# A two-layer graph network with masked attention: one cyclic order by hand for all engines, norms on ScalarE, adj turned straight from DRAM

## The chip, the cores and the metric

The kernel runs on one core of a Trainium2 chip. A core has TensorE (PE in the profile; PEld are its weight loads), VectorE (DVE), ScalarE (ACT), GpSimd (POOL) and SyncE (SP), which here only issues DMAs. Each engine executes its own instructions in the order in which they were put into its stream, and waits on semaphores for what other engines or DMAs have to deliver. The metric is the time of one launch on the device in microseconds, the median of several runs.

## The reference

There are B = 64 independent elements. Each has a matrix x of N = 256 tokens by F = 512 features, and adj, 256 by 256, non-negative and mostly zero. All is float32. Two layers are applied, each followed by a residual sum and a layer norm without learned factors:

```python
# layer 0
deg = sum(adj, axis=-1)
agg = einsum('bij,bjf->bif', adj, x) / maximum(deg, 1e-6)
x   = layernorm(x + relu(concatenate([x, agg]) @ W0.T))
# layer 1: 8 heads of 64
q, k, v = x @ Wq.T + bq, x @ Wk.T + bk, x @ Wv.T + bv
scores  = einsum('bhqd,bhkd->bhqk', q, k) * 64 ** -0.5
attn    = softmax(scores * (adj + adj))
x       = layernorm(x + (attn @ v) @ Wo.T + bo)
```

The kernel computes adj·(x·W) instead of (adj·x)·W in layer 0. The division by the degree belongs to a row of the sum, so it can be applied to the rows of adj beforehand or to the rows of the product afterwards.

## The kernel before

**Tiling.** A tile has 128 partitions (P). The 256 tokens of an element are NT = 2 groups of 128, the 512 features FC = 4 groups of 128. Tokens are put on the partitions in an order of blocks of L = 32[...]: a full transpose is made of a DMA that moves the blocks to their places and a VectorE transpose inside them.

**Products.** The four big projections (L for layer 0, Q for queries and keys, V for values, O for the output) are each done by a seven-product scheme of Winograd's kind (`winograd`): two blocks of tokens by two blocks of features, seven block products, numbered 1 to 7, instead of eight. The sums of weight blocks are made once (`sum_blocks`, L125). The sums of token blocks are made per element by GpSimd (`token_sums`, L214): s1 to s4, in tiles named sums. The products run in the order 5, 1, 3, 6, 2, 7, 4 into three PSUM accumulators, called c, a and b (p0c, p0a, p0b for L; pq, pv, po for Q, V, O). An accumulator goes on being added to after a part has been copied out: product 3 adds onto c after product 5 was copied out of it, 6 onto a after 1, 7 after 6, and 4 after the result of 7 was joined. So TensorE has to wait for each of these copies (`keep`: ScalarE for L, Q, V; VectorE for O, L489) and of the joins (`join`, VectorE, L236).

In the profile, one product of 128 by 512 in float32 is two MATMUL rows; one of the seven steps of L has 4 rows, of Q 16, of V and O 4 of half the width.

**Stages of an element b.**

- `prepare`: turn x (z_x to xT, L274), its token sums, degree and 1/degree (L280 to L283), adj scaled row by row by 1/degree (`an`, L286), written to DRAM (way_a, L185) and fetched back turned by blocks (z_a, L193), then turned by VectorE into aT (L197).
- `project0` and `layer0`: the L products into oy, of which one half is x·W and the other is to be multiplied by adj; two neighbour sums pm (L323) of four wide products together; add (L327), relu and residual (L328), layer norm (`layer_norm`, L171 to L181) into x1; x1 goes to DRAM (way_x) and comes back twice: turned (`turn1`) and plain, as rest (`fetch_x1`), to which GpSimd adds the bias (L342).
- `queries_keys`, `values`: Q and V.
- `attend`: for each of four pairs of heads, scores sc (L416), times adj into s (L428), maximum of each row (L435), four exponentials on ScalarE with a running sum (L438), reciprocal (L446), four scalings by it on VectorE (L448), a transpose of the blocks (L205), out to DRAM (way_s, L207) and back as sT (L209).
- `context`: attention times v (pc, L462), copied to ctxT (L469), token sums of it.
- `project1`, `finish`: O, the second layer norm, output in eight DMAs (L498).

A layer norm takes the statistics on VectorE (L174, L176), adds epsilon and takes the power -1/2 on GpSimd (L178, L180), and applies both on VectorE (L181).

**Order.** `iteration(i)` (L502) works on several elements at once: scores of element i, layer 0 of i + 2, queries, keys and values of i + 1, output of i - 1, preparation of i + 3. Only TensorE's order is written by hand (L541): its instructions run in the order in which the program names them. For VectorE, ScalarE, GpSimd and the DMA queue on SP the framework's scheduler picks the order, by priorities and its own estimates. All DMAs of the loop leave from the one queue on SP. Most tiles have between two and four buffers[...].

Of the kernel before, what the change touches and what calls it, by code (L numbers as in the profile page):

```python
# [7 lines left out]
F32 = mybir.dt.float32  # L8
# [6 lines left out]
DEG_EPS = 1e-6  # L15


@with_exitstack
def kernel(
# [29 lines left out]

    nc = tc.nc  # L50
# [7 lines left out]
    A = P // L  # L58

# [8 lines left out]
    def bank(name):  # L68
        return banks.tile([P, F], F32, tag="ps", name=name)

    def token_rows(tile, dram, a):

        rows = dram.rearrange("(a t l) f -> a l t f", a=A, t=NT)
        return tile[a * L : (a + 1) * L], rows[a]

    xs, adjs, zxs = {}, {}, {}
    loaded = set()

    def load_turned(b):
        if b >= B or b in loaded:  # L80
            return
        loaded.add(b)
        zxs[b] = sb.tile([P, A, NT, F // A], F32, tag="z", name=f"z_x_{b}", bufs=3)
        for a in range(A):
            nc.sync.dma_start(
                out=zxs[b][a * L : (a + 1) * L].rearrange("m b t k -> m (b t) k"),
                in_=x[b, :, a * P : (a + 1) * P].rearrange("(g m) k -> m g k", m=L),
            )

    def load_rows(tiles, dram, b, tag, bufs):  # L90
        if b >= B or (tag, b) in loaded:
            return
        loaded.add((tag, b))
        tiles[b] = sb.tile([P, NT, dram.shape[2]], F32, tag=tag, name=f"{tag}_{b}", bufs=bufs)
        for a in range(A):
            dst, src = token_rows(tiles[b], dram[b], a)
            nc.sync.dma_start(out=dst, in_=src)
# [12 lines left out]
    def load_blocks(queue, dst, dram, swapped=False, natural=False):  # L110

        for blk, kh, nh in ((B11, 0, 0), (T3, 0, 1), (B21, 1, 0), (B22, 1, 1)):
            nh ^= swapped
            cols = dram[:, nh * G : (nh + 1) * G]
            if natural:
                rows = cols.rearrange("(c p) o -> p c o", p=P)
                queue.dma_start(out=dst(slice(None), blk), in_=rows[:, 2 * kh : 2 * kh + 2])
                continue
            rows = cols.rearrange("(a c l) o -> a l c o", a=A, c=FC)
            for a in range(A):  # L120
                queue.dma_start(
                    out=dst(slice(a * L, (a + 1) * L), blk), in_=rows[a, :, 2 * kh : 2 * kh + 2]
                )
# [5 lines left out]
    load_turned(0)  # L129
    load_blocks(nc.scalar, lambda p, k: w0[p, k, :, 1], w0t[F:])  # L130
    load_blocks(nc.sync, lambda p, k: w0[p, k, :, 0], w0t[:F])
    for b in range(2):
        load_turned(b)
        load_rows(adjs, adj, b, "adj", 4)
        load_rows(xs, x, b, "x", 3)
    bqk = const.tile([P, 2, FC], F32, name="bqk")
    nc.scalar.dma_start(out=bqk[:, 0], in_=bq)
    nc.scalar.dma_start(out=bqk[:, 1], in_=bk)
    bvT = const.tile([P, FC], F32, name="bvT")
    nc.scalar.dma_start(out=bvT, in_=bv.rearrange("o (c p) -> p (o c)", p=P))  # L140
    bo_sb = const.tile([P, F], F32, name="bo_sb")
    nc.scalar.dma_start(out=bo_sb, in_=bo.to_broadcast([P, F]))
    load_blocks(nc.sync, lambda p, k: wo[p, k], wot, natural=True)
    load_blocks(nc.sync, lambda p, k: wqk[p, k, :, 0], wqt, swapped=True)
    load_blocks(nc.sync, lambda p, k: wqk[p, k, :, 1], wkt, swapped=True)
    load_blocks(nc.sync, lambda p, k: wv[p, k], wvt)
    sum_blocks(nc.vector, w0.rearrange("p k c m o -> p k (c m o)"))

    def later_weights():
# [3 lines left out]
        sum_blocks(nc.vector, wqk.rearrange("p k c m o -> p k (c m o)"))  # L153

        bv_all = sb.tile([P, FC, P], F32, tag="h", name="bv_all", bufs=3)
        nc.vector.tensor_copy(bv_all, bvT.unsqueeze(2).to_broadcast([P, FC, P]))
        ps = bank("p_bv")
# [11 lines left out]
        sum_blocks(nc.gpsimd, wv.rearrange("p k c o -> p k (c o)"))  # L169

    def layer_norm(dst, src, tag):  # L171

        stats = small.tile([P, 6], F32, tag="stats", name=f"stats_{tag}")
        nc.vector.bn_stats(stats, src)  # L174
        mv = small.tile([P, 2], F32, tag="mv", name=f"mv_{tag}")
        nc.vector.bn_aggr(mv, stats)  # L176
        ve = small.tile([P, 1], F32, tag="ve", name=f"ve_{tag}")
        nc.gpsimd.tensor_scalar(ve, mv[:, 1:2], LN_EPS, None, ALU.add)  # L178
        rstd = small.tile([P, 1], F32, tag="rstd", name=f"rstd_{tag}")
        nc.gpsimd.tensor_tensor(rstd, ve, neg_half, ALU.pow)  # L180
        nc.vector.tensor_scalar(dst, src, mv[:, 0:1], rstd, ALU.subtract, ALU.mult)  # L181

    def outward(src, C, tag):
        way = bounce.tile([NT * A, L, A * C * L], F32, tag=f"way{C}", name=f"way_{tag}", bufs=5)
        nc.sync.dma_start(out=way.rearrange("(t b) m k -> (b m) t k", t=NT), in_=src)  # L185
        return way

    def transposed(dst, way, tag):

        C = dst.shape[1]  # L190
        z = sb.tile([P, NT, A, C * L], F32, tag="z", name=f"z_{tag}", bufs=3)
        for a in range(A):
            nc.sync.dma_start(  # L193
                out=z[a * L : (a + 1) * L].rearrange("m t b k -> m (t b) k"),
                in_=way[:, :, a * C * L : (a + 1) * C * L].rearrange("g m k -> m g k"),
            )
        nc.vector.transpose(  # L197
            dst.rearrange("p c t (b m) -> p (t b) c m", m=L),
            z.rearrange("p t b (c l) -> p (t b) c l", l=L),
        )  # L200

    def transposed_s(dst, s, tag):

        flat = s.rearrange("p a c r l -> p (a c r l)")
        nc.vector.transpose(flat, flat)  # L205
        way = bounce.tile([A, L, A, NT * 2 * NT * L], F32, tag="way_s", name=f"way_{tag}", bufs=4)
        nc.sync.dma_start(out=way.rearrange("b l a k -> (b l) (a k)"), in_=flat)  # L207
        for a in range(A):
            nc.sync.dma_start(  # L209
                out=dst[a * L : (a + 1) * L].rearrange("l b c r m -> l b (c r m)"),  # L210
                in_=way[:, :, a].rearrange("b l k -> l b k"),
            )

    def token_sums(src, tag):  # L214


        def block(t, kh):
            return src[:, 2 * kh : 2 * kh + 2, t]

        sums = sb.tile([P, 4, 2, P], F32, tag="sums", name=f"sums_{tag}", bufs=3)  # L220
        s1, s2, s3, s4 = (sums[:, k] for k in range(4))
        nc.gpsimd.tensor_tensor(s1, block(1, 0), block(1, 1), ALU.add)  # L222
        nc.gpsimd.tensor_tensor(s2, s1, block(0, 0), ALU.subtract)
        nc.gpsimd.tensor_tensor(s3, block(0, 0), block(1, 0), ALU.subtract)
        nc.gpsimd.tensor_tensor(s4, block(0, 1), s2, ALU.subtract)
        return {1: block(0, 0), 2: block(0, 1), 3: s4, 4: block(1, 1), 5: s1, 6: s2, 7: s3}
# [3 lines left out]
    def winograd(multiply, keep, part, psums):  # L230


        pa, pb, pc = psums

        def join(ps, t, n):
            nc.vector.tensor_tensor(part(t, n), ps, part(t, n), ALU.add)  # L236

        multiply(5, pc, True)
        keep(pc, 1, 1)
        yield  # L240
        multiply(1, pa, True)
        keep(pa, 0, 0)
        yield
        multiply(3, pc, False)
        yield
        multiply(6, pa, False)
        keep(pa, 0, 1)
        yield
        join(pc, 0, 1)
        multiply(2, pb, True)  # L250
        join(pb, 0, 0)
        yield
        multiply(7, pa, False)
        join(pa, 1, 1)
        yield
        multiply(4, pa, False)
        keep(pa, 1, 0)
        yield

    def by_turns(order, works):  # L260

        for name in order:
            if name in works:
                next(works[name])

    xTs, aTs, x1Ts, qks, vs, sTs, cTs = {}, {}, {}, {}, {}, {}, {}
    xSs, x1Ss, cSs, ways, rests = {}, {}, {}, {}, {}

    def prepare(b):

        xT = sb.tile([P, FC, NT, P], F32, tag="xT", name=f"xT_{b}")
        z = zxs.pop(b)
        for t in range(NT):
            nc.vector.transpose(  # L274
                xT[:, :, t].rearrange("p c (b m) -> p b c m", m=L),
                z[:, :, t].rearrange("p b (c l) -> p b c l", l=L),
            )
        xSs[b] = token_sums(xT, f"x_{b}")
        deg = small.tile([P, NT], F32, tag="deg", name=f"deg_{b}")
        nc.vector.tensor_reduce(deg, adjs[b], AX.X, ALU.add)  # L280
        nc.vector.tensor_scalar(deg, deg, DEG_EPS, None, ALU.max)
# [3 lines left out]
        for t in range(NT):  # L285
            nc.vector.tensor_scalar(an[:, t], adjs[b][:, t], rdeg[:, t : t + 1], None, ALU.mult)  # L286
# [292 lines left out]
```

## Time and profile before

| | before |
|---|---|
| median of 3 runs | 3511.33 us (3509.74 to 3514.02) |
| span of the profiled execution | 3508.7 us |
| instructions | 51138 |
| TensorE's granted clock, mean | 0.989 |
| DMA | 530.14 MB, 58.2% of the 16 engines' span for the queue on SP |

After its start the program runs in equal turns, one for each element. To read it, the turn is the unit: what each engine does in a turn, where TensorE stands still in it, and what ended that. In the rows of groups, the columns are line, engine, operation, output and input, shapes, number of instructions, then busy time and mean duration in ns, then the idle time of the engine ahead of them and what ended it.

### The profile page before, as it was taken

Reading aid. Unit: us, or ns where it says so; the run is one execution under the profiler, and the core shown is the slowest. Engines: PE = TensorE matmul, PEld = TensorE weight load, DVE = VectorE, ACT = ScalarE, POOL = GpSimd, SP = SyncE. Lnnn points to the kernel's source line nnn. Section 1 sums busy time; section 2 is a strip of 40 time slices with the busy share of each in tenths; the row PEclk is TensorE's granted clock in tenths of the full one; section 3 lists DMA queues with packets and bytes.
Section 4 is the critical chain, followed back from the end, with each engine's and each line's share of the span. In section 5 each row is a group of like instructions: output and inputs, shape, how many; then the busy total and the mean of one; then the engine's idle time right before and its main releaser. Section 6 shows DMA issues by size and latency. Waiting matters only on the chain.

```text
span 3508.7 us, 51138 instructions
## 1 busy us (share of the span) xinstructions
PE 3185.1 (91%) x17168; PEld 2216.8 (63%) x17168; DVE 2692.0 (77%) x4943; ACT 1083.1 (31%) x3713; POOL 952.1 (27%) x1421
## 2 busy tenths in 40 slices
PE   4989999999999999999999999999999999999996
PEld 2665665666666666656656656666666666566565
DVE  4668778787787787787787787877877877877875
ACT  0323333233232332332333332332323323333332
POOL 2222231331322322322322313313223223223222
PEclk8999999999999999999999999999999999999998
DMA  5555655655665565556556556656655665565554
GB/s 149 133 135 141 158 157 143 159 155 146 158 158 150 156 157 154 153 148 159 157 143 158 156 143 160 153 149 157 159 150 155 155 157 153 146 158 156 143 136 130
DMA packets 519686, 530.14 MB, mean 151 GB/s; under 512 B 119936, under 2 KB 420992, under 8 KB 519424
## 3 DMA queue, kind: packets, MB, share of 16 engines
q1 hardware_dynamic: 517184, 525.55, 58.2%
q8 instruction: 137, 2.24, 0.3%
q10 hardware_dynamic: 2240, 1.32, 0.2%
q14 instruction: 125, 1.02, 0.1%
HBM read 308.55 MB, written 218.10 MB: 150 GB/s over the span
## 4 chain that ended last, share of the span: by engine, by line
DVE 34%; PE 33%; ACT 8%; POOL 7%; issue 6%; SPq 5%; DMA 5%; DVEq 0%; ACTq 0%; POOLq 0%
PE p0a L301 7%; ACT s L438 7%; DVE s L428 7%; PE pqa L355 7%; DVE nmax L435 6%; DVE s L448 5%; PE pqc L355 4%; PE p0b L301 3%; POOL rstd L180 3%; DMA way_a<-an 2%; DVE stats L174 2%; PE sc L416 2%; DVE x1T L197 2%; SPq L209 2%; PE pva L384 2%
## 5 line engine op out<-in xcount | busy, mean ns | idle before, releaser
L438 ACT ACTIVATE s<-s,nmax 128x256 f32<-128x256 f32 x1024 | 507.6, 497 | 609.1 <-DVE nmax L435 609.1
L371 ACT ACTIVATE qk<-pqa,bqk 128x128 f32<-128x128 f32 x768 | 219.0, 368 | 842.2 <-PE pqa L355 842.2
L222 POOL TENSOR_TENSOR sums_x<-x1T 128x256 f32<-128x256 f32 x64 | 46.7, 729 | 1453.7 <-DVE rtotal L446 1378.1
L448 DVE TENSOR_SCALAR s<-s,rtotal 128x256 f32<-128x256 f32 x1024 | 393.4, 446 | 6.5
L355 PE MATMUL pqc<-sums_x,wqk 128*128 128x128 f32 x2048 | 259.1, 280 | 98.8 <-POOL sums_x L222 98.7
L428 DVE TENSOR_TENSOR s<-sc,adj 128x512 f32<-128x512 f32 x512 | 327.9, 681 | 27.0 <-PE sc L416 26.9
L355 PEld LDWEIGHTS pqc<-sums_x,wqk 128*128 128x128 f32 x2048 | 247.0, 194 | 153.2 <-POOL sums_x L222 148.5
L205 DVE STREAM_TRANSPOSE s<-s 128x1024 f32<-128x1024 f32 x256 | 317.8, 1241 | 6.3
L301 PE MATMUL p0c<-w,sums_x 128*128 128x512 f32 x512 | 253.6, 618 | 73.4 <-ACT oy L314 59.4
L435 DVE TENSOR_REDUCE nmax<-s 128x4 f32<-128x1024 f32 x256 | 312.2, 1219 | 8.5
L178 POOL TENSOR_SCALAR ve<-mv 128x1 f32<-128x1 f32 x256 | 56.9, 222 | 871.9 <-DVE mv L176 871.9
L181 DVE TENSOR_SCALAR x<-oy,mv,rstd 128x512 f32<-128x512 f32 x128 | 124.6, 974 | 217.5 <-POOL rstd L180 217.5
L301 PE MATMUL p0a<-w,sums_x 128*128 128x512 f32 x512 | 246.9, 604 | 24.2 <-ACT oy L314 24.2
L323 PE MATMUL pm<-oy,aT 128*128 128x512 f32 x512 | 238.6, 609 | 31.1 <-DVE aT L197 29.5
L416 PE MATMUL sc<-qk 64*128 64x256 f32 x2048 | 255.2, 389 | 0.0
L355 PEld LDWEIGHTS pqa<-x1T,wqk 128*128 128x128 f32 x2048 | 248.4, 192 | 10.3 <-DVE qk L236 3.9
L462 PE MATMUL pc<-sT,v 128*64 128x256 f32 x2048 | 250.6, 386 | 3.7 <-DMA sT<-way_s 3.7
L355 PEld LDWEIGHTS pqa<-sums_x,wqk 128*128 128x128 f32 x2048 | 248.6, 192 | 6.5
L355 PE MATMUL pqa<-x1T,wqk 128*128 128x128 f32 x2048 | 249.8, 275 | 2.5 <-DVE qk L236 2.5
L355 PE MATMUL pqa<-sums_x,wqk 128*128 128x128 f32 x2048 | 249.3, 275 | 0.0
L301 PE MATMUL p0a<-w,xT 128*128 128x512 f32 x512 | 247.3, 605 | 1.6 <-DVE oy L236 1.6
L416 PEld LDWEIGHTS sc<-qk 64*128 64x128 f32 x2048 | 187.4, 186 | 88.7 <-issue 71.6
(89 smaller groups left out, 5351.2 us busy)
## 6 DMA issues: line engine op xcount, KB each, us to landing
way_s<-s SPq DMA_DIRECT2D x256, 512.0 KB, 3.2
sT<-way_s SPq DMA_DIRECT2D x1024, 128.0 KB, 3.9
z_x<-in_x_dram SPq DMA_DIRECT2D x256, 128.0 KB, 3.9
x<-in_x_dram SPq DMA_DIRECT2D x256, 128.0 KB, 2.7
way_x<-x SPq DMA_DIRECT2D x64, 512.0 KB, 3.1
z_x<-way_x SPq DMA_DIRECT2D x256, 128.0 KB, 3.1
rest<-way_x SPq DMA_DIRECT2D x64, 512.0 KB, 5.8
out_dram<-h SPq DMA_DIRECT2D x512, 64.0 KB, 1.7
```

The source lines that it names most:

```text
L181: nc.vector.tensor_scalar(dst, src, mv[:, 0:1], rstd, ALU.subtract, ALU.mult)
L205: nc.vector.transpose(flat, flat)
L301: nc.tensor.matmul(ps, lhsT=left[k][:, c], rhs=w0[:, WEIGHTS[k], c], start=start and c == 0, stop=True, skip_group_check=True,)
L323: nc.tensor.matmul(ps, lhsT=aT[:, j, t], rhs=oy[:, 1, j], start=(j == 0), stop=(j == NT - 1))
L355: nc.tensor.matmul(ps[:, m, j], lhsT=wqk[:, WEIGHTS[k], c, m, j * P : (j + 1) * P], rhs=left[k][:, c], start=start and m == j == c == 0, s ...
L371: nc.scalar.activation(part(t, n)[:, m, j], ps[:, m, j], AF.Identity, bias=bqk[:, m, c : c + 1])
L416: nc.tensor.matmul(scs[hp, j][:, t], lhsT=qk[d, 0, hp, t * P : (t + 1) * P], rhs=qk[d, 1, hp].rearrange("d (t b m) -> d b t m", t=NT, m=L) ...
L428: nc.vector.tensor_tensor(rows[:, j * NT : (j + 1) * NT], scs[hp, j].rearrange("p t (k l) -> p t k l", l=L), aj.rearrange("p t (k l) -> p ...
L435: nc.vector.tensor_reduce(nmax, rows, AX.XY, ALU.max, negate=True)
L438: nc.scalar.activation(rows[:, r], rows[:, r], AF.Exp, bias=nmax[:, r : r + 1], accum_out=total[:, r : r + 1],)
L448: nc.vector.tensor_scalar(rows[:, r], rows[:, r], rtotal[:, r : r + 1], None, ALU.mult)
L462: nc.tensor.matmul(ps[j * D : (j + 1) * D, n], lhsT=vs[b][:, c, h * D : (h + 1) * D], rhs=sT[:, :, c, j * NT : (j + 1) * NT].rearrange("p ...
```

## The change

Four things change together.

1. **One cyclic order by hand.** The stages become named steps, and a table `PLAN` lists them in the order in which every engine gets them. Each entry is a step and an offset: `L5+2` is product 5 of L for element i + 2. All engines and the DMA queue are now ordered by hand (`tc.manual_schedule()` without a list of engines): an engine's instructions run in the order of the table, whatever is ready earlier. The rows of the table begin with a step of TensorE; the other steps in a row belong to other engines. TensorE's own order changes as well: the scores of the four pairs of heads are spread (Sa, Sb; Sc, Sd), and the neighbour sums AY0, AY1 come ahead of Q.
2. **Norms and softmax scaling move to ScalarE.** The four scalings of each pair of heads (step na to nd) and the four applications of a layer norm (AYn, ln) become ACTIVATEs with a scale, and for the norms a bias, for each partition. GpSimd makes the bias, one more small operation for each norm.
3. **adj is turned straight from DRAM** (step Dza), without `an` and its way through DRAM; 1/degree is applied when the neighbour sum is added (AYa).
4. **Buffers.** x, xT, z, s, sT, sums and h1 get names of their own with one buffer each; adj has four, v two, the DRAM tiles for x1 five. The output leaves in four DMAs. Of the weights, those of the queries load from ScalarE's queue.

The names of the steps: S scores, m times adj, M maximum, e and f exponentials, r reciprocal, n scaling, T transpose, Dw and Ds out to DRAM and back, C context and c its copy; Lk, Qk, Vk, Ok copies and Lj, Qj, Vj, Oj joins of a product; AY neighbour sum, AYa add and relu, AYb statistics, AYp factors, AYn norm; lb, lp, ln the same of the last norm; xS, yS, cS token sums; Dx, Dzx, Dza, Dadj loads; Dway, Dz1, Drest the ways of x1.

The core of the diff:

```diff
+PLAN = """
+    Sa+0 c0-1 lp1-2 Dx+2
+    Sb+0 ma+0 xS2+2
+    L5+2 ln1-2 Dsd-1 Ma+0 xS4+2
+    L1+2 Lk5+2 x1T+1 Dsc-1 ea+0 mb+0
+    L3+2 yS1+1 Dza+3 Lk1+2 yS2+1 fa+0 Mb+0 yS4+1
+    L6+2 lb0-2
+    L2+2 Lk6+2 lp0-2 eb+0 bo-1
+    L7+2 Lj2+2 fb+0 Lj3+2 ra+0
+    Sc+0 Lj7+2 na+0
+    Sd+0 mc+0
+    L4+2 ln0-2 rb+0 md+0 Dout-2
+    C1a-1 Lk4+2 Mc+0 nb+0
+    C1b-1
+    AY0+2 Md+0 ec+0
+    AY1+2 AYa0+2 fc+0 AYb0+2
+    Q5+1 ed+0 rc+0 Ta+0 c1-1
+    V5+1 AYa1+2 cS1-1 Qk5+1
+    Q1+1 cS2-1 AYb1+2 cS4-1 Vk5+1
+    V1+1 Qk1+1 Tb+0 cS3-1
+    Q3+1 yS3+1 Vk1+1 Dwb+0 AYp0+2 Dwa+0 nc+0 Dadj+4
+    O5-1 AYp1+2
+    Q6+1 Tc+0
+    O1-1 Ok5-1 Qk6+1
+    Q2+1 Ok1-1 Dsb+0 fd+0 Qj3+1
+    V3+1 Dsa+0 AYn0+2 rd+0 Qj2+1
+    Q7+1 nd+0
+    O3-1 Qj7+1 AYn1+2
+    V6+1 Td+0 Dway+2
+    Q4+1 Vk6+1 deg+4 xT0+3
+    O6-1 Qk4+1 Vj3+1
+    V2+1 Ok6-1 xT1+3
+    O2-1 Dz1+2 xS3+3
+    V7+1 xS1+3
+    O7-1 Vj7+1 Dwd+0 Dwc+0
+    V4+1 Oj7-1 Oj2-1
+    O4-1 Vk4+1 aT+3
+    C0a+0 Ok4-1 Vj2+1 Drest+0
+    C0b+0 Oj3-1 Dzx+4 lb1-1
+"""
...
-        nc.vector.tensor_scalar(dst, src, mv[:, 0:1], rstd, ALU.subtract, ALU.mult)
+    def norm_factors(name, b):
+        mv = held[f"mv_{name}", b]
+        nc.gpsimd.tensor_scalar(mv[:, 1:2], mv[:, 1:2], LN_EPS, None, ALU.add)
+        nc.gpsimd.tensor_tensor(mv[:, 1:2], mv[:, 1:2], neg_half, ALU.pow)
+        nc.gpsimd.tensor_scalar(mv[:, 0:1], mv[:, 0:1], mv[:, 1:2], -1.0, ALU.mult, ALU.mult)
+    def norm_apply(name, b, dst, src):
+        mv = held[f"mv_{name}", b]
+        nc.scalar.activation(dst, src, AF.Identity, bias=mv[:, 0:1], scale=mv[:, 1:2])
...
-        an = sb.tile([P, NT, N], F32, tag="h", name=f"an_{b}", bufs=3)
-        for t in range(NT):
-            nc.vector.tensor_scalar(an[:, t], adjs[b][:, t], rdeg[:, t : t + 1], None, ALU.mult)
-        transposed(aTs[b], outward(an, NT, f"a_{b}"), f"a_{b}")
+    @step("Dza")
+    def _(b):
+        z = tile_of("za", b, [P, A, NT, N // A])
+        for a, part in groups():
+            nc.sync.dma_start(
+                out=z[part].rearrange("m b t k -> m (b t) k"), in_=turned_rows(adj[b], a, N // A)
+            )
...
-            nc.vector.tensor_tensor(h, ps, h, ALU.add)
+            nc.vector.scalar_tensor_tensor(h, held[f"AY{t}", b], rdeg, h, ALU.mult, ALU.add)
...
-                nc.vector.tensor_scalar(rows[:, r], rows[:, r], rtotal[:, r : r + 1], None, ALU.mult)
+                nc.scalar.activation(
+                    rows(b)[:, r], rows(b)[:, r], AF.Identity, scale=of("total", b)[:, r : r + 1]
+                )
...
-    with tc.manual_schedule(engines={mybir.EngineType.PE}):
-        for i in range(-3, B + 1):
-            iteration(i)
+    with tc.manual_schedule():
+        run("Dzx", 0)
+        first_weights()
+        run("Dza", 0)
+        run("Dadj", 0)
+        run("Dx", 0)
+        run("Dadj", 1)
+        run("Dadj", 2)
+        run("Dzx", 1)
+        more_loads()
+        for i in range(-6, B + 6):
+            for name, ahead in plan:
+                if name == "Q5" and i + ahead == 0:
+                    later_weights()
+                if name == "bo" and i + ahead == 0:
+                    last_weights()
+                run(name, i + ahead)
```

## The prediction

> **What bounds the kernel now.** I read the busy shares first, then TensorE's timeline over one turn of the loop, then the table of waits, then the price rows.
>
> ```profile
> PE 3185.1 (91%) x17168; PEld 2216.8 (63%) x17168; DVE 2692.0 (77%) x4943; ACT 1083.1 (31%) x3713; POOL 952.1 (27%) x1421
> ```
>
> TensorE is the fullest engine, and nobody else is near it. But 91% does not say that only 9% can be had. Here is TensorE in the turn from 1705.74 us (start, length, instruction, number, and in brackets the idle time before it):
>
> ```profile
> 1707.62 2.00 PE L416 MATMUL sc<-qk 64*128 64x256 f32 x16
> 1709.54 1.98 PE L301 MATMUL p0c<-w,sums_x 128*128 128x512 f32 x4
> 1711.36 1.88 PE L301 MATMUL p0a<-w,xT 128*128 128x512 f32 x4
> 1714.16 1.96 PE L301 MATMUL p0c<-w,sums_x 128*128 128x512 f32 x4 [0.92 <-ACT oy L314]
> 1716.52 1.98 PE L301 MATMUL p0a<-w,sums_x 128*128 128x512 f32 x4 [0.40 <-ACT oy L314]
> 1718.34 1.88 PE L301 MATMUL p0b<-w,xT 128*128 128x512 f32 x4
> 1720.06 1.88 PE L301 MATMUL p0a<-w,sums_x 128*128 128x512 f32 x4
> ...
> 1727.59 3.70 PE L323 MATMUL pm<-oy,aT 128*128 128x512 f32 x8
> 1732.61 2.05 PE L355 MATMUL pqc<-sums_x,wqk 128*128 128x128 f32 x16 [1.32 <-POOL sums_x L222]
> 1734.50 1.03 PE L384 MATMUL pvc<-wv,sums_x 128*128 128x256 f32 x4
> 1735.36 1.95 PE L355 MATMUL pqa<-x1T,wqk 128*128 128x128 f32 x16
> ...
> 1745.96 1.95 PE L355 MATMUL pqa<-sums_x,wqk 128*128 128x128 f32 x16
> 1749.02 1.13 PE L384 MATMUL poc<-wo,sums_c 128*128 128x256 f32 x4 [1.11 <-DVE h L489]
> ```
>
> Read starts, not lengths. A step of four wide products takes 1.72 us to the next start when nothing stops it (1718.34 to 1720.06), a Q step 1.79, a V or O step 0.86. The next turn begins at 1759.01, so a turn is 53.27 us. From the first score step (107.69) to that of element 62 (3409.04) 62 turns took 3301.35 us: 53.25 each, regular. The ends are 107.7 us of start and 99.7 us of tail.
>
> Four holes recur. p0a to p0c takes 2.80 (1.08 too much), p0c to p0a 2.36 (0.64), pm to pqc 5.02 (1.56 above 3.46), pqa to poc 3.06 (1.27)[...]. Who is waited for:
>
> ```profile
> POOL sums_x L222 <- DVE rtotal L446: 1378.1, 59, 23.5
> PE pqc L355 <- POOL sums_x L222: 98.7, 60, 11.4
> PE poc L384 <- DVE h L489: 72.7, 61, 6.6
> PE p0c L301 <- ACT oy L314: 59.4, 63, 2.9
> ```
>
> In every case the helper engine was busy with something less urgent: eight exponentials ahead of the copy of p0c; softmax scaling (L448) around the turn of x1; h (L489) behind work that waited for ACT. Thus order and helper load bound the turn, not arithmetic. The last-ending chain says the same: DVE 34%, PE 33%.
>
> [...]49.51 us busy in this turn, yet the sum of undisturbed steps is 48.04 (below). [...]L448 lies between 305 and 1357 ns, L328 between 648 and 1215, L181 up to 1580. [...]SP waited 771.7 us in all with L207 for L205.
>
> **Part by part.**
>
> *TensorE's work is unchanged, only reordered.* One stall-free turn from the starts above: S 2x1.92, L 1.82 + 5x1.72 + 1.92, C 2x1.88, AY 3.46, Q 7x1.79 = 12.53, V and O 14x0.865 = 12.11. Sum **48.04 us**.
>
> *Removed from VectorE per element:* 16 softmax scalings (393.4/64 = 6.15 us), four norm applications (194.4/64 = 3.04), two an scalings (0.63). Its turn falls from 41.9 to about 33 us.[...] The multiply by 1/degree enters the existing add (L327 becomes the two-scalar form, still one pass, 0.69): nothing.
>
> *Added to ScalarE.*
>
> ```profile
> L438 ACT ACTIVATE s<-s,nmax 128x256 f32<-128x256 f32 x1024 | 507.6, 497 | 609.1 <-DVE nmax L435 609.1
> L448 DVE TENSOR_SCALAR s<-s,rtotal 128x256 f32<-128x256 f32 x1024 | 393.4, 446 | 6.5
> L181 DVE TENSOR_SCALAR x<-oy,mv,rstd 128x512 f32<-128x512 f32 x128 | 124.6, 974 | 217.5 <-POOL rstd L180 217.5
> ```
>
> The 16 scalings become ACTIVATEs of L438's shape. Lower price: 0.40 us apiece (497 ns less overlap); upper: 0.50, the pitch of the exponentials with their accumulator reads. I take 0.50: 8 us.[...] ScalarE's turn goes from 16.9 to about 28 of 48 us. GpSimd gets a third small operation in each norm, 0.22 us as L178: 0.9 us.
>
> *Removed from the DMA queue:* the way_a write (256 KB per element) and its landing ahead of z_a (2.7 us); adj is turned straight from DRAM with the same 256-byte runs, and out goes in four issues, not eight. 46 issues of about 0.46 us = 21 us of the turn: free, off the path. It also cuts the chain an - way_a - z_a - aT, which ran through every turn.
>
> *Order.* Lay the steps at the starts of a stall-free turn: L5 1.92, L1 3.74, L3 5.46, L6 7.18, L2 8.90, L7 10.62, Sc 12.34, L4 14.26, C1a 16.18, AY0 18.06, Q5 21.52, V5 23.31, Q1 24.18, Q3 26.83, O5 28.62, Q6 29.49, Q7 34.80, O3 36.59, V6 37.45, Q4 38.32, V7 42.70, O7 43.57, V4 44.43, O4 45.30, C0a 46.16. A result can be read 0.2 us after the next step starts (pob 1701.09, next step 1701.95, VectorE's add 1702.16). Then fill each helper in the plan's order.
> - VectorE: ma 1.15-2.4, Ma to 3.6, x1T to 4.8, mb, Mb to 7.3, lb0 to 8.2, Lj2 from 9.9 (L2 ready 10.8) to 11.5, Lj3, ra, Lj7 12.55-13.2: L4 at 14.26 has 1 us to spare. mc, md, Mc, Md to 18.8; AYa0, AYb0 20-22.2; Ta, AYa1, AYb1, Tb to 27.8; Tc about 30; Ok5 31, Ok1, Qj3, rd, Qj2, Qj7 36.8-37.5 for Q4 at 38.32; Td, deg, xT0, Vj3, Ok6 41.6, xT1 42.3, Vj7 43.8-44.2 for V4 at 44.43; Oj7 44.65-45.05 for O4 at 45.30; aT, Ok4, Vj2, Oj3, lb1 to 0.5 of the next turn.
> - ScalarE: ln1 to 2.4; Lk5 3.95-4.5 for L3 at 5.46; ea; Lk1 5.7-6.3 for L6 at 7.18; fa; Lk6 9.1-9.7 for L7 at 10.62; eb, fb, na, ln0 to 15.2; Lk4 to 17.0 for AY0 at 18.06; nb, ec, fc, ed, c1 to 22.5; Qk5 23.5-24.7; Qk1 to 27.4 for Q6; nc to 29.7; Qk6 to 32.6; fd, AYn0, nd, AYn1 to 37.0; Vk6, Qk4, Vk4.
> - GpSimd: xS4 by 3.1 for L3, yS by 7.1, lp0 and bo to 12.1, cS1 by 22.7 for O5, yS3 by 26.
> - Queue: x1 leaves at 37.1, lands 40.7, comes back turned about 45.5, is wanted at 3.6 of the next turn (6 us spare). Dsc is issued by about 6.6 behind Drest, Dzx, Dx, Dsd and lands by 11; C1a wants it at 16.18. Dsb behind Dwb's landing (31) is back by 36 for C0a at 46. One buffer per tile suffices at these times.
> - Banks: 24 tiles of PSUM in a turn, three rounds of eight. The dearest hand-over is Oj3's bank (free at 47.6) to Sb at 48.04 + 0.96.
>
> Every TensorE wait finds its releaser done; the thinnest are V4 and O4 with 0.2 us. A wait met so late stops early weight loading (length 1.13 against 1.03, 0.1 us each). I add 0.3 us: **48.3 us a turn**. The bound below is 48.04; above, two holes of the present size remaining, 50.3.
>
> *Ends.* Start: the first wide product still waits for w0 (14 us). The aT of element 0 came at 58 because its bounce queued behind 50 us of weight issues; now za is ahead of them, and wq's 16 issues go to ACT's queue. L0 to 27, AY0 to 32, x1 back turned at about 52 (its issues still stand behind wk, wv, wo), AY for element 1 to 60, six us of scaling wqk, Q and V 18.6: the first score step at **88** instead of 107.7 (75 to 108). The first turn lacks O and C1 (-8.0) and has the bias product (+3.6). Tail: 95, about as before (99.7), since it is the latency of softmax, bounce, O.
>
> Sum: 88 + (48.3 - 8.0 + 3.6) + 61x48.3 + 95 = **3173**, say 3175.
>
> **Rivals.**
> (A) The strict order catches on something that I laid too early, and two of four holes live on elsewhere: 50.3 a turn, 3173 + 62x2.0 = 3297. For it: VectorE and ScalarE cannot overtake any longer, and V4/O4 have 0.2 us. Against: 15 us of VectorE free in each turn.
> (B) Waits take the place of waits: about 53 a turn again, the start alone gains, near 3490. For it: two engines that had slack of 11 and 36 us still made 5 us of holes. Against: those holes came from urgent work behind unurgent, which the plan separates.
> (C) Slower: single buffers in an ordered queue put one bounce into the turn, a landing of 3.2 plus 2.9 of waiting on SP's longest z_a wait: 54.4 a turn, 3173 + 62x6.1 = 3551. For it: x, z, s and sT lose their spare buffers. Against: the shortest time to spare I find on the queue is about 5 us.
>
> **How the numbers follow.** Forecast 0.67, A 0.21, B 0.03, C 0.09. Lower end: 48.04 throughout and a start at 75 give 3173 - 16 - 13 = 3144, less a little for the tail: 3130. The upper end reaches to A: 3300. Faster by over 0.2% takes forecast, A and most of B: 0.90; same 0.01; slower 0.09.
>
> **What would show it.** The turn between first score steps near 48.3; the four PE holes gone from the waits; L448's rows on ACT at 0.40 to 0.50; VectorE near 2150 us busy in all, ACT near 1800; no way_a; V4 and O4 with 1.13 lengths. I am wrong if a turn exceeds 49.5: then look at which row PE waits for, first at V4/O4, the copies Lk, and Sa's banks.

## The result, and the profile after

| | before | after |
|---|---|---|
| median, 4 runs each, side by side | 3511.24 us (3509.74 to 3514.02) | 3184.52 us (3182.38 to 3186.09) |
| ratio | | 0.9068, 95% interval 0.9053 to 0.9084 |
| span of the profiled execution | 3508.7 us | 3181.5 us |
| first score step | 107.69 us | 95.53 us |
| turn, mean of 62 | 53.25 us | 48.19 us |
| from element 62's score step to the end | 99.6 us | 98.3 us |

The forecast was 3175 us. Of the 327.2 us by which the span shrank, 62 x 5.06 = 313.7 are the turn, 12.2 the start and 1.3 the tail. The mean of 62 includes a first turn without the output projection (41.18 us) and a second one with the bias product (51.70); every turn after them takes 48.25 us.

The busy shares after:

```profile
PE 3112.6 (98%) x17168; PEld 2237.0 (70%) x17168; DVE 2119.2 (67%) x3599; ACT 1699.8 (53%) x4993; POOL 1016.5 (32%) x1677
```

The number of matmuls is unchanged. TensorE's timeline around the place where the hand-ordered kernel now begins a turn (start, length, instruction; idle time would stand in brackets):

```profile
1728.58 1.03 PE L349 MATMUL Va<-wv,x1T 128*128 128x256 f32 x4
1729.44 1.03 PE L349 MATMUL Oa<-wo,cT 128*128 128x256 f32 x4
...
1734.20 1.98 PE L349 MATMUL Lc<-w,xS 128*128 128x512 f32 x4
1736.02 1.88 PE L349 MATMUL La<-w,xT 128*128 128x512 f32 x4
1737.74 1.88 PE L349 MATMUL Lc<-w,xS 128*128 128x512 f32 x4
...
1750.42 3.70 PE L450 MATMUL AY<-oy,aT 128*128 128x512 f32 x8
1753.95 1.95 PE L378 MATMUL Qc<-yS,wqk 128*128 128x128 f32 x16
```

There is no bracket left in the turn. TensorE's rows of a whole turn, set beside a turn before, also show that its own order is all but the old one: the score steps already stood in two groups and pm ahead of Q. Only one pair of steps has changed places: V6 (1721.61) now stands ahead of Q4 (1722.47), where Q4 (1749.99) stood ahead of V6 (1751.77). So the list of the change, which has a new order for TensorE too, says too much there: what got a new order are the three helper engines and the DMA queue.

Lc to La to Lc takes 1.82 and 1.72 us, where p0a to p0c took 2.80. AY to Q takes 3.53, where pm to pqc took 5.02. V4 and O4, the two steps with the least to spare, have 1.03, not the 1.13 of a late wait, which both have in the kernel before (1756.96 and 1757.95): their weight loads begin at 1728.39 and 1729.25, 0.19 us ahead of them. The table of TensorE's waits has no row any more that comes back in each turn (total us, times, longest):

```profile
PE Lc L349 <- DVE w L170: 14.3, 1, 14.3
PE pc L608 <- DMA sTc<-wsc: 8.4, 1, 8.4
...
PE Oc L349 <- POOL cS L290: 6.0, 2, 4.6
```

All of these lie in the start or in the tail. Together TensorE's waits come to 59 us, against 316 before. TensorE itself makes up 96% of the chain that ended last (before 33%). For the 62 turns alone (stretch, its length, TensorE's busy time, matmuls, granted clock, DMA share, GB/s), first before, then after:

```profile
107.69:3409.04 3301.35, 3063.11 (x16574) 1.00 0.59 152
95.53:3083.15 2987.62, 2987.10 (x16589) 1.00 0.63 163
```

Of the 313.7 us, 237.7 are idle time that has gone. The other 76.0, or 1.2 us a turn, are busy time, most of it beside the holes: the step ahead of a hole counts with its whole length (pm 3.70 us) and not with the pitch to a next step (3.46), and the one behind it begins together with its weight loads (poc at 1749.02, 1.13 us), where a step without a wait begins 0.1 to 0.2 us behind them (poa at 1699.37, its loads at 1699.15, 1.03 us).

The work that moved, as groups on ScalarE:

```profile
L571 ACT ACTIVATE sa<-sa,totala 128x256 f32<-128x256 f32 x256 | 109.1, 497 | 47.2 <-DVE totala L566 47.2
...
L442 ACT ACTIVATE x<-oy,mv 128x512 f32<-128x512 f32 x128 | 104.1, 814 | 6.5 <-POOL mv L438 6.5
```

Four scalings in a row take 1.70 us, so one costs about 0.40. The norm takes 814 ns in layer 0 and 808 at the end of an element; what the forecast of ScalarE's turn counted for it was an estimate of mine.

### The profile page after: what moved, and what is told of

It reads as the page before. It is cut to its first block, busy times and chain, and to the rows that moved or that the text cites. A ratio compares the mean times of both kernels' runs of the same rounds, so it can differ in the third digit from the quotient of the medians.

```text
span 3181.5 us, 51140 instructions
## 1 busy us (share of the span) xinstructions
PE 3112.6 (98%) x17168; PEld 2237.0 (70%) x17168; DVE 2119.2 (67%) x3599; ACT 1699.8 (53%) x4993; POOL 1016.5 (32%) x1677
## 4 chain that ended last, share of the span: by engine, by line
PE 96%; DMA 1%; SPq 1%; ACT 1%; DVE 1%; issue 0%; POOL 0%; ACTq 0%; POOLq 0%; DVEq 0%
PE Qa L378 14%; PE La L349 14%; PE pc L608 7%; PE Qc L378 7%; PE AY L450 7%; PE Lc L349 7%; PE Oa L349 7%; PE Va L349 7%; PE Qb L378 4%; PE Oc L349 4%; PE Vc L349 3%; PE Lb L349 3%; PE sca L525 2%; PE scc L525 2%; PE Vb L349 2%; PE Ob L349 2%
## 5 line engine op out<-in xcount | busy, mean ns | idle before, releaser
L378 PEld LDWEIGHTS Qc<-yS,wqk 128*128 128x128 f32 x2048 | 250.3, 193 | 39.1 <-issue 34.6
L349 PE MATMUL Lc<-w,xS 128*128 128x512 f32 x512 | 252.7, 617 | 25.2 <-DVE w L170 14.3
L378 PE MATMUL Qc<-yS,wqk 128*128 128x128 f32 x2048 | 251.3, 276 | 4.2 <-POOL mv L438 3.4
L349 PE MATMUL La<-w,xT 128*128 128x512 f32 x512 | 251.0, 613 | 3.4 <-DVE oy L330 3.4
L378 PEld LDWEIGHTS Qa<-x1T,wqk 128*128 128x128 f32 x2048 | 248.6, 192 | 7.2 <-DVE qk L330 0.6
L378 PEld LDWEIGHTS Qa<-yS,wqk 128*128 128x128 f32 x2048 | 248.6, 192 | 6.5
L378 PE MATMUL Qa<-x1T,wqk 128*128 128x128 f32 x2048 | 249.5, 275 | 0.0
L378 PE MATMUL Qa<-yS,wqk 128*128 128x128 f32 x2048 | 249.3, 275 | 0.0
L349 PE MATMUL La<-w,xS 128*128 128x512 f32 x512 | 241.5, 594 | 0.0
L450 PE MATMUL AY<-oy,aT 128*128 128x512 f32 x512 | 236.8, 605 | 0.0
```

Source lines behind the costliest of these rows:

```text
L349: nc.tensor.matmul(ps[:, :width], lhsT=left(k, b, c), rhs=w[:, WEIGHTS[k], c], start=first and c == 0, stop=True, skip_group_check=True,)
L378: nc.tensor.matmul(ps.rearrange("p (m j q) -> p m j q", m=2, j=2)[:, m, j], lhsT=wqk[:, WEIGHTS[k], c, m, j * P : (j + 1) * P], rhs=left_y ...
L450: nc.tensor.matmul(ps, lhsT=held["aT", b][:, j, t], rhs=held["oy", b][:, 1, j], start=(j == 0), stop=(j == NT - 1),)
```

## The experiments

The change has three parts: the order, the load moved to ScalarE, and the way of adj. The experiments take them apart, then try parts of the order, then the two ends. The new buffers go with the order in all of them and were not tried alone. Turns are means over 62, read as in the table above.

### The order without the move to ScalarE

The kernel after, with scaling and norms back on VectorE:

```diff
-                nc.scalar.activation(rows(b)[:, r], rows(b)[:, r], AF.Identity, scale=...)
+                nc.vector.tensor_scalar(rows(b)[:, r], rows(b)[:, r], ..., None, ALU.mult)
...
-        nc.gpsimd.tensor_scalar(mv[:, 0:1], mv[:, 0:1], mv[:, 1:2], -1.0, ALU.mult, ALU.mult)
-        nc.scalar.activation(dst, src, AF.Identity, bias=mv[:, 0:1], scale=mv[:, 1:2])
+        nc.vector.tensor_scalar(dst, src, mv[:, 0:1], mv[:, 1:2], ALU.subtract, ALU.mult)
```

> The changed kernel's hand order, but the softmax scaling and the four norm applications per element back on VectorE (adj still comes straight from DRAM). Theory 'order': VectorE has about 33 us of work in a turn of 48.2, and 6.2 + 3.0 us more still fit between its deadlines, so the turn stays within 0.5 us of 48.2 and the time is 3180 to 3230 us. Rival 'load': the holes came from VectorE's amount of work; then at least half of the gain is lost and the time is 3320 to 3450 us.

Measured: 3185.61 us (3185.24 to 3188.33), ratio 0.9073 (0.9059 to 0.9086), a turn of 48.19. VectorE is busy for 2480.2 us (78%), ScalarE for 1111.0 (35%). That is the time of the kernel after: under the hand order the move to ScalarE is worth nothing that can be measured. VectorE's scalings took 344 to 358 ns here and 446 before, the norm of layer 0 took 536 and 974, the last norm 544 and 546. So the scalings and the norm of layer 0 got shorter without being taken off VectorE. For the norm this is not the hand order's doing alone: in adj_direct_alone below, planned as before, it took 557.

### The move to ScalarE without the order

The kernel before with both the load moved and adj turned straight, planned as before:

```diff
-                nc.vector.tensor_scalar(rows[:, r], rows[:, r], rtotal[:, r : r + 1], None, ALU.mult)
+                nc.scalar.activation(rows[:, r], rows[:, r], AF.Identity, scale=rtotal[:, r : r + 1])
...
-        nc.vector.tensor_scalar(dst, src, mv[:, 0:1], rstd, ALU.subtract, ALU.mult)
+        nc.gpsimd.tensor_scalar(mv[:, 0:1], mv[:, 0:1], rstd, -1.0, ALU.mult, ALU.mult)
+        nc.scalar.activation(dst, src, AF.Identity, bias=mv[:, 0:1], scale=rstd)
...
-        transposed(aTs[b], outward(an, NT, f"a_{b}"), f"a_{b}")
+        rdegs[b] = rdeg
+                in_=adj[b][:, a * (N // A) : (a + 1) * (N // A)].rearrange("(g m) k -> m g k", m=L),
...
-            nc.vector.tensor_tensor(h, ps, h, ALU.add)
+            nc.vector.scalar_tensor_tensor(h, ps, rdegs[b][:, t : t + 1], h, ALU.mult, ALU.add)
```

> The kernel before with its old order and scheduler, but softmax scaling and norms on ScalarE, adj turned straight from DRAM and 1/degree applied to the sum. Theory 'order': the copies of L stand behind still more ScalarE work, so their holes stay or grow (1.1 + 0.6 us and more), the hole ahead of Q shrinks; turn 51 to 55 us, time 3370 to 3600 us. Rival 'load': relieving VectorE is what counts; turn below 50, time 3180 to 3300 us.

Measured: 3592.03 us (3587.04 to 3596.37), ratio 1.0223 (1.0206 to 1.0240): slower, a turn of 54.74, although VectorE's busy time fell from 2692.0 to 2094.9 us. TensorE's waits:

```profile
PE pqa L366 <- ACT qk L382: 108.0, 59, 2.0
PE p0c L312 <- ACT oy L325: 82.5, 63, 2.2
PE poc L395 <- DVE h L500: 65.7, 59, 1.1
```

The hole at pqc has gone and one at pqa stands in its place, now behind ScalarE. Two edits are mixed here, so the second was also made alone.

### adj turned straight, without the rest, and the reverse

The last two hunks above, alone on the kernel before:

> The kernel before with one part of the change alone: adj turned straight from DRAM, 1/degree applied to the sum; scaling and norms stay on VectorE, the order is the old one. Theory: aT was waited for only once, so the turn stays at 53.0 to 53.6 us; with a start up to 20 us shorter 3485 to 3530 us in all. Rival (the chain through the bounce held up the queue and through it x1 and the turned scores): 52 us a turn or less, under 3440 us.

And the kernel after with only this undone (`an`, its way out to DRAM and back, and a plain add of the sum), in the hand order:

```diff
-    Q4+1 Vk6+1 deg+4 xT0+3
+    Q4+1 Vk6+1 deg+4 an+4 xT0+3
...
-    C0b+0 Oj3-1 Dzx+4 lb1-1
+    C0b+0 Oj3-1 Dzx+4 Dwaya+4 lb1-1
...
-            nc.vector.scalar_tensor_tensor(h, held[f"AY{t}", b], rdeg, h, ALU.mult, ALU.add)
+            nc.vector.tensor_tensor(h, held[f"AY{t}", b], h, ALU.add)
```

> The kernel after with one part undone: adj is again scaled by 1/degree on VectorE, written out and fetched back turned (two TENSOR_SCALARs, five more DMA issues and their landing in every turn), and the sum is added without the factor; the order by hand stays. Theory (the order is worth all of the turn, the path of adj has over half a turn to spare): a turn of 48.2 to 48.4 us, 3178 to 3205 us in all, the rest of the difference in the start, where element 0's adj takes one more trip. Rival (the shorter path of adj is part of the gain): 49.5 us a turn or more, over 3260 us.

Measured: with the detour under the hand order 3193.72 us (3193.25 to 3196.58), ratio 0.9094 (0.9081 to 0.9108), a turn of 48.19 again; the first score step is at 106.5 instead of 95.53. So turning adj straight is worth the 11 us of the start and nothing in the turn.

Alone under the old order it made the kernel slower: 3587.47 us (3582.12 to 3589.67), ratio 1.0209 (1.0192 to 1.0226), a turn of 54.56. Both theories missed that. With the load moved as well (load_alone) the time is nearly the same, 3592 against 3587 with ranges that overlap, so here too the move was worth nothing that can be measured. As the two kernels wait in different places, this does not show that their losses have one cause. TensorE's timeline in a turn of adj_direct_alone:

```profile
1777.70 1.95 PE L365 MATMUL pqa<-sums_x,wqk 128*128 128x128 f32 x16
1782.37 1.17 PE L394 MATMUL poc<-wo,sums_c 128*128 128x256 f32 x4 [2.72 <-DVE h L499]
1783.34 3.58 PE L365 MATMUL pqa<-x1T,wqk 128*128 128x128 f32 x16
1786.74 1.03 PE L394 MATMUL pva<-wv,sums_x 128*128 128x256 f32 x4
```

The hole ahead of pqc has gone, and the one at poc has grown from 1.11 us to 2.72. Its chain: h waited for GpSimd's sum of rest and bias, and that for rest from DRAM, whose issue at 1773.79 stood in the queue behind twelve fetches of turned scores. It was issued 9.4 us after the start of pqc (1764.37); in the kernel before it was 5.0. The holes of the 62 turns hardly change in sum (238.2 us before, 252.2 here). What changes is the step behind the hole: start to start it takes 3.40 us instead of 1.79. TensorE's busy time in the 62 turns grows by 67.4 us to 3130.5; with 14.0 us more of holes these are the 62 x 1.31 = 81 us that the turns take longer. Over the whole run the Q steps are busy for 59 us and the poc steps for 30 us longer than before, other steps a little shorter.

This is the clock: it was 0.961 on average, 0.989 before, and in the slow step it was 0.50. In the traces of before and after its changes lie 3.41 us or a whole multiple of that apart (6.83, 10.24, 13.65, 30.72), so TensorE's busy time is read in stretches of that length here, around this hole and around one of 2.25 us that was not followed by a slow step (columns as above):

```profile
1779.92:1783.34 3.42, 0.97 (x5) 1.00 0.97 274
1783.34:1786.75 3.41, 3.41 (x18) 0.50 0.78 171
...
1506.86:1510.27 3.41, 1.48 (x9) 1.00 1.01 287
1510.27:1513.68 3.41, 3.41 (x23) 1.00 0.64 131
```

The first hole leaves TensorE busy for 28% of its stretch, and the clock is halved in the next one. The other one (1506.54 to 1508.79) lies across two stretches and leaves 43% in the second, and the clock stays.

Of the 58 holes of 2.06 to 3.84 us at poc in this trace, 52 were followed by slow steps, and six (2.06 to 2.42) by steps of full speed. In load_alone 37 of the 58 holes of 1.83 to 2.04 us at pqa were followed by slow steps: from pqa to pqb took 2.75 us behind the other 21, and at least 4.01 behind these.

To see whether the queue's place for rest was the cause, its fetch was issued from ScalarE's queue, with everything else as in adj_direct_alone:

```diff
-        nc.sync.dma_start(out=rests[b], in_=ways.pop(b).rearrange(...))
+        nc.scalar.dma_start(out=rests[b], in_=ways.pop(b).rearrange(...))
```

> The kernel before with adj turned straight from DRAM and 1/degree on the sum, as in adj_direct_alone, and the fetch of rest issued from ScalarE's queue instead of SyncE's. In adj_direct_alone TensorE waited 2.7 us a turn for h at the second O product, because rest landed 2.8 us later against the Q steps than in the kernel before, its fetch standing behind twelve fetches of turned scores, and the next Q step then ran 3.4 us instead of 1.8. Theory (the fetch's place in the queue is the cause): that wait falls to 1.2 us a turn or less, the slow Q step goes, a turn of 52.0 to 53.4 us, 3420 to 3525 us in all. Rival (the re-planned order of VectorE and GpSimd is the cause, wherever rest comes from): the wait at O stays over 2 us, a turn of 54 us or more, over 3560 us.

Measured: 4173.05 us (4169.09 to 4181.60), ratio 1.1877 (1.1858 to 1.1897). The wait at poc is gone from the table, but the scheduler made another plan for the helper engines around the moved issue, and there VectorE does the turn of x1 (at 1790.07) behind the next element's layer norms (1781 to 1790):

```profile
PE pqc L365 <- POOL sums_x L222: 690.8, 61, 13.6
```

Eleven us a turn, and the clock falls to 0.896. Both theories missed. The run does not settle alone how much of adj_direct_alone's loss the queue makes, since one edit moved everything. It does show what the old order is: a plan in which an edit of one line moves the turn by 10 us.

### Which engines have to be ordered

The kernel after with only TensorE's order kept by hand, as before the change (helpers_by_scheduler); the same with scaling and norms on VectorE (pe_order_alone); and the reverse, the kernel before with all engines held to the order in which its program names its operations (old_program_order). The edit of the first two, which the third makes the other way round:

```diff
-    with tc.manual_schedule():
+    with tc.manual_schedule(engines={mybir.EngineType.PE}):
```

> The changed kernel with only TensorE's order by hand; VectorE, ScalarE, GpSimd and the DMA queue are ordered by the framework's scheduler again. Theory 'order of the helpers': with TensorE's new order and the new division of work alone some holes come back, turn 49.5 to 55 us, time 3260 to 3600 us. Rival 'TensorE's new order and the load are enough': 3180 to 3215 us.

> TensorE's new order alone: helpers ordered by the scheduler, softmax scaling and norms on VectorE; of the change only TensorE's order, the buffers and the direct turn of adj are left. Theory 'order of the helpers': about as slow as the kernel before, 3380 to 3700 us. Rival 'TensorE's order': 3180 to 3260 us.

> The kernel before with all engines in the order in which its program names the steps, nothing else changed. Theory: an order by hand is worth what its order is; here VectorE waits for the exponentials of each pair of heads in turn and TensorE's joins stand behind that, turn 58 to 70 us, time 3800 to 4600 us. Rival 'a fixed order in itself helps': below 3500 us.

Measured: helpers_by_scheduler 3729.19 us (3727.17 to 3732.61), ratio 1.0620 (1.0604 to 1.0635); pe_order_alone 3411.13 us (3409.45 to 3415.15), ratio 0.9715 (0.9700 to 0.9729); old_program_order 6172.73 us in one run. The first two differ from after and order_alone in this one line. With the turns of the kernels that turn adj straight:

| order | scaling and norms on VectorE | on ScalarE |
|---|---|---|
| all by hand | 48.19 | 48.19 (after) |
| the program after, TensorE by hand, the rest planned | 51.90 | 57.03 |
| the program before, TensorE by hand, the rest planned | 54.56 | 54.74 |

So the fixed order of the helpers is worth 3.7 us of a turn with the work on VectorE and 8.8 with it on ScalarE. That this program is faster under the planner than the one before, 51.90 against 54.56, can hardly be TensorE's order, which differs by one pair of steps; the buffers and the order in which the program names the helpers' steps differ too, and which of them counts was not tried.

helpers_by_scheduler is slower than all that was expected of it. Its ScalarE around one Q product, then TensorE:

```profile
1715.32 0.81 ACT L442 ACTIVATE x<-oy,mv 128x512 f32<-128x512 f32 x1 [5.36 <-POOL mv L438]
1716.04 1.12 ACT L396 ACTIVATE qk<-Qc,bqk 128x128 f32<-128x128 f32 x4
```

```profile
1717.30 3.43 PE L378 MATMUL Qc<-yS,wqk 128*128 128x128 f32 x16 [5.86 <-ACT qk L396]
```

ScalarE stood idle for 5.36 us in front of the norm, whose factors were late, while the copy out of Qc, whose step had ended when Vc began at 1707.77, stood behind it; TensorE waited 5.86 us, and then ran the step at about half rate (granted clock 0.55). The same move of load that is harmless by hand costs 5.1 us a turn under this plan, and 0.2 under that of the program before: what an operation put on ScalarE costs depends on whether it is put ahead of an urgent copy.

In old_program_order TensorE's longest wait is of the same kind:

```profile
PE p0c L301 <- ACT oy L314: 1229.1, 62, 20.8
```

ScalarE's copy stands behind exponentials that wait for VectorE. With the waits for h ahead of poc (578.0) and for oy ahead of pm (417.2) it makes 36 us a turn, and the clock is 0.783. An order kept strictly is worth what the order is worth; I expected the direction, but too small a size.

### One urgent copy put behind less urgent work

In the kernel after, ScalarE's copy out of the fourth L product (Lk4) is put behind three exponential steps of two exponentials each:

```diff
-    C1a-1 Lk4+2 Mc+0 nb+0
+    C1a-1 Mc+0 nb+0
...
-    AY0+2 Md+0 ec+0
+    Md+0 ec+0 fc+0 ed+0 Lk4+2
+    AY0+2
```

> The changed kernel with one step of ScalarE misplaced: the last copy of L (Lk4) stands behind six exponentials (ec, fc, ed) instead of ahead of the scaling of pair b. Nothing is added. Theory 'urgent behind unurgent': the first neighbour sum waits for it, 2.8 to 3.5 us in every turn; turn 51.0 to 51.7, time 3355 to 3405 us. Rival: ScalarE is idle 20 us of a turn, that absorbs it; 3180 to 3200 us.

Measured: 3304.59 us (3303.32 to 3304.86), ratio 0.9411 (0.9398 to 0.9424), a turn of 50.14: 1.95 more than after, not 2.8 to 3.5.

```profile
1719.92 1.12 PE L451 MATMUL AY<-oy,aT 128*128 128x512 f32 x2
1722.65 2.84 PE L451 MATMUL AY<-oy,aT 128*128 128x512 f32 x6 [1.60 <-ACT oy L368]
```

The kind is as expected: one recurring wait, in every turn, for this copy (101.5 us in 62 turns). The size was off because AY0's first wide product needs only the block of tokens that was ready earlier; TensorE works for one product, 0.86 us, before it waits.

### The two ends

short_start issues wq's blocks from SP, and the blocks of wv and wo from GpSimd, loads za of element 1 ahead of the weights, and makes the sums of wqk at the first x1T instead of the first Q5. short_ends has this too, and another order for the last elements. Of the cut below, the last lines are of short_ends alone:

```diff
-        load_blocks(nc.scalar, lambda p, k: wqk[p, k, :, 0], wqt, swapped=True)
...
-        run("Dadj", 2)
         run("Dzx", 1)
+        run("Dza", 1)
+        run("Dadj", 2)
         more_loads()
...
-                if name == "Q5" and i + ahead == 0:
+                if name == "x1T" and i + ahead == 0:
                     later_weights()
...
+                if name == "Drest" and i + ahead >= B - 3:
+                    run("Dsd", i)
+                    run("Dsc", i)
```

> The changed kernel with another start: the query weights are issued by SP instead of ScalarE, the value and output weights by GpSimd, adj of element 1 is fetched ahead of the weights, and the scaling and sums of the query and key weights stand ahead of the first turn of x1. Theory: L of element 0 no longer waits for ScalarE's 36 DMA issues (third product at 19.5 instead of 24.35 us), x1 is back some 6 us earlier and Q waits for no weights: first score step at 82 to 90 us instead of 95.5, time 6 to 13 us less, 3171 to 3179 us, turn unchanged. Rival: the start is set by the weights' bytes, and nothing changes by more than 3 us.

> short_start plus another order in the last turns: in the last three elements the attention comes back ahead of rest, and in the last turn the transposes of pairs c and d and their ways through DRAM stand ahead of the output projection. Theory: the tail from the score step of element 62 shrinks from 98.4 to 86 to 92 us; time 14 to 22 us below the changed kernel, 3162 to 3172 us. Rival: the tail is a chain of latencies that the order does not touch; the same as short_start within 3 us.

Measured: short_start 3178.07 us (3176.36 to 3179.59), ratio 0.9051 (0.9039 to 0.9064); first score step at 87.53, turn 48.19, tail 99.4. short_ends 3176.66 us (3176.24 to 3178.12), ratio 0.9048 (0.9035 to 0.9060); 90.18, 48.19, 98.4. The shorter start is worth 6.5 us in the medians and 8.0 at the first score step, and both kernels are faster than the kernel after. The tail's order is worth 1 us at most: C1a of the last element but one comes sooner, but the last element still takes 31 us from its last score step (3122.08) to the last of its C1 steps (3153.53), which waits for turned scores, and 23 more to the end. Latencies make up most of it, but not all: rest was now fetched last (issue at 3148.94), and GpSimd's token sums for the last O, whose input was ready at 3155.2, stood behind the bias on rest until 3156.85. That short_ends has its first score step 2.65 us later than short_start, with the same code up to there, lies for 2.06 us in adj of element 1, for which VectorE waited until 32.75 us instead of 30.69; why it landed later stays open.

## Why the prediction was right, and where it was not

**The turn.** Right to 0.1 us (48.3 forecast, 48.25 measured from the third turn on), and by its own sum: undisturbed steps at the pitch between starts. The 0.3 us that I had added for late waits stand for something else, since nothing was late; that they fit so well is luck. The difference to 48.04 lies in changes from one kind of step to another, which the price list took at the undisturbed pitch: AY to Q 3.53 for 3.46, L7 to the score step 1.81 for 1.72, O4 to C0a 0.95 for 0.865, together 0.25, against 0.04 less elsewhere.

**"Order and helper load bound the turn".** Half wrong. Order, with the buffers that go with it, gives the whole turn (order_alone, adj_detour), and load alone gives nothing (load_alone against adj_direct_alone). The reading that each helper was busy with something less urgent was right, though of the eight exponentials named ahead of the copy of p0c four stood there (1711.47 to 1713.45) and four ahead of that of p0a; the inference that less work on VectorE would help was not. I had counted four holes by whom TensorE waited for, and then took the helper's busy share for a part of the cause, when only the place of one operation in its queue was. Against rival A I named 15 us of free time on VectorE; order_alone has some 48.2 - 2480.2/64 = 9.4 us and no hole, so that argument was not what carried it.

**The path of adj.** Forecast as off the path, and it is so in the turn. In the start it is worth 11 us.

**The rivals.** A did not come: V4 and O4, with 0.2 us to spare, held. B is what the same edits do under the old order: in adj_direct_alone and load_alone a wait takes the place of the one removed. I gave B little because the plan separates urgent from less urgent work, and that is the reason that the runs bear out. C did not come: single buffers and the one queue make no recurring wait.

**The start.** The step that failed: 88 us forecast, 95.53 measured. "L0 to 27, AY0 to 32" were 36.7 and 40.3. I laid out the loads, and put L0 at its undisturbed pitch, 12.3 us from 14.26. It took 22.5. Left out were the engines' own order in the start and the rate at which TensorE runs there:

```profile
22.37 1.28 ACT L367 ACT_TABLE_LOAD   x1 [22.37 <-DMA adj<-in_adj_dram]
23.66 0.59 ACT L367 COPY oy<-Lc 128x512 f32<-128x512 f32 x1
```

```profile
24.35 3.75 PE L349 MATMUL Lc<-w,xS 128*128 128x512 f32 x4 [3.81 <-issue]
...
32.52 0.69 DVE L330 TENSOR_TENSOR oy<-Lb,oy 128x512 f32<-128x512 f32 x1 [1.22 <-PE Lb L349]
```

The 36 issues on ScalarE's queue end at 22.3, so the first copy out of Lc came at 23.66, and TensorE stood still for 3.81 us ahead of the third L product. The join of L7 held L4 for another 0.79: in the start no score steps lie between the two. The other 5.5 us are steps at a lower rate. The first took 3.55 us to the next start instead of 1.82, the third 3.54 instead of 1.72, and in the third the granted clock was 0.50 (for the first step the trace has no record of it). From there the lateness stayed: AY of element 1 came at 67.18 instead of 60, the scaling and sums of wqk took 2.3 us less than I had set, Q and V 2.6 us more. With the helpers planned the program has its first score step at 91.50 (helpers_by_scheduler) and 92.50 us (pe_order_alone): in the start the fixed order costs a few us.

short_start shows that ScalarE's issues are not the only limit, and that the fixed order has another one behind them. There the third product starts at 19.78, yet AY0 at 37.96 (after: 36.73), because VectorE takes the degree of element 1, whose adj lands late, ahead of the joins:

```profile
30.69 0.69 DVE L274 TENSOR_REDUCE deg<-adj 128x2 f32<-128x512 f32 x1 [6.22 <-DMA adj<-in_adj_dram]
34.39 3.78 PE L351 MATMUL La<-w,xT 128*128 128x512 f32 x4 [7.57 <-DVE oy L332]
```

In the kernel after, VectorE was through with this by 31.3, and its first join waited for TensorE (the row at 32.52). short_start's gain comes later: AY of element 1 at 64.40 instead of 67.18 (2.8 us), although its L began 2.0 us later. Its joins stand behind the turn of x1, which ended sooner against them, so L4 waits 0.79 us for a join and not 2.60, and two steps of that L are not slow. Q5 starts 3.5 us after AY and not 7.1, the sums of wqk being done (3.6 us), and it runs at full rate (1.6 us). These are the 8.0 us. x1 itself was turned 1.6 us earlier (59.04 instead of 60.65), not 6 as short_start's theory had it, so that its time came out right is in part luck. The forecast of 88 was reached by a kernel with another start than the one forecast.

**Sizes.** "Only reordered" was too much for TensorE's work, since the turn differs by one pair of steps. The scaling on ScalarE costs the lower of my two prices, 0.40. With it ScalarE is busy for 1700 us instead of about 1800. VectorE has 2119 for about 2150. Relu and residual take as long as before, a mean of 929 ns (L463) for 922 (L328). They are not on the path. The tail took 98.3 us for 95.

## What to carry to other kernels

When TensorE waits in every turn for helpers that have time to spare, look at what stands ahead of the awaited operation in the helper's stream: here putting all helpers' steps into one cyclic order, together with its buffers, was worth all 5 us of each turn, while TensorE's own order hardly changed, and taking 361 of VectorE's 2480 us away was worth nothing. Sum TensorE's undisturbed starts to know what such an order can reach; it told the turn to 0.1 us. Don't judge a part of such a change by trying it alone under the planner, where an edit of one line moved the turn by 10 us: try it again under the fixed order.

## What the runs showed of the hardware

- A hole of some 2 us cost more than itself in some places and not in others. Behind 52 of the 58 holes of 2.06 to 3.84 us at poc in adj_direct_alone, and behind 37 of the 58 of 1.83 to 2.04 us at pqa in load_alone, TensorE's steps were slow; behind the other six and 21 they ran at full speed. In late_copy the steps behind the 61 holes of 1.60 us all took 2.84 us, and the granted clock was 0.991 on average.
- In the kernel before, the granted clock of the 62 turns fell once: it was 0.50 from 232.58 to 242.82 us, around the end of a hole of 10.52 us, and it fell behind none of the 183 holes of 0.5 to 1.57 us.
- In adj_direct_alone the steps behind the holes took 1.4 us a turn longer, where the whole turn took 1.31 longer; in the turn of helpers_by_scheduler shown above a Q step of 3.43 us stood behind a hole of 5.86.
- VectorE's scalings took 446 ns in the kernel before, 344 to 358 in order_alone, and 356 to 776 by pairs of heads in pe_order_alone; the norm of layer 0 took 974, 536 and 546. The same scaling took 344 to 776 ns, and the same norm 536 to 974, in kernels that order the work around it differently. What makes the difference was not tried.
